# The sends of a second half chained in fours, and a quarter of the dense expert moved forward, in a decoder layer with a mixture of experts

## The chip, the cores and the metric

The kernel runs on one core of one Trainium2 chip. The metric is the time of one execution on the device in microseconds (us), the median of several runs. Lower is better. Inside a core, engines work side by side, each through its own instructions in order: PE (TensorE, matrix products; PEld is its loading of weights), DVE (VectorE), ACT (ScalarE), POOL (GpSimd) and SP (SyncE, which here issues DMAs). They wait for each other by semaphores. PEclk in the profile is the clock that TensorE was granted, as a share of the full one.

## The reference

One decoder layer over 1024 tokens of width 256 in float32: self attention, cross attention, and a mixture of experts, each behind a layer norm and with a residual. The change touches only the last:

```python
scores = softmax(xt @ Wg.T)                       # 16 experts
topi = top 4 of the experts of the best 2 of 4 groups
combine[t, topi] = scores[t, topi]
h = silu(einsum('td,eid->eti', xt, W1)) * einsum('td,eid->eti', xt, W3)   # 176 wide
y = einsum('etd,te->td', einsum('eti,edi->etd', h, W2), combine)
z = silu(xt @ Ws1.T) * (xt @ Ws3.T) @ Ws2.T       # the shared expert
return y + z
```

## The kernel before

**Tokens and halves.** The 1024 tokens are kept as eight tiles `x[i]` of 128 tokens by 256; tiles 0 to 3 are the first half, 4 to 7 the second. Routing, the shared expert and one of the 16 routed experts, the dense one (the last, `w_last`), are computed half by half. The dense expert is computed for all tokens of a half and added with each token's weight for it (`add_last`, L952), in four quarters of 256 tokens: `dense_hidden` computes the hidden layer of a quarter, `dense_output` its outputs and the adds. Before the change the two quarters of the first half are done early, and those of the second half, (1,0) and (1,1), at the end of the kernel.

**Sends.** The other 15 experts get their tokens through memory. `send` (L837) scatters the rows of a half with indirect DMAs on POOL: for each of a token's four choices k, four DMAs of 128 rows (i = 0 to 3), each row going into its expert's slots in `xd`; 16 for each half, in the order of k. `side_by_side` (L243) tells the scheduler that the sends don't depend on each other, so none waits for another. `sent_for[k]` keeps the sends of choice k.

**Experts.** The loop over e (L1353) is a software pipeline. For each expert:

- `expert_inputs(e)` loads its 384 slots (`xr`, SP queue, L1255), behind all sends of the choices 0 to min(3, e): expert 0's load waits for choice 0 alone, expert 3's and all later ones for all four. PE transposes the rows (six transposes, L1265), and ACT (L112) and DVE (L113) split them into a high and a low part, `xs`.
- `expert_weights` loads the weights (640 KB, SP queue, L277) and splits them too: a cast on ACT (L278) and subtractions on DVE or POOL (L283).
- `expert_hidden` computes 18 matmuls of 128x384, the silu on ACT (L1283, L1286), the product on DVE (L1284, L1287), and the parts `hp` of the hidden layer.
- `send_outputs` computes the outputs with 15 matmuls, copies them (L1299), and scatters them into `yd` by three indirect DMAs on POOL (L1304).

In step e of the loop, the inputs of e, the hidden layer of e − 1 and the outputs of e − 2 are written down. For e = 1 and 2 `expert_hidden` is called ahead of the next expert's inputs, and the inputs are tied behind its matmuls (`up_done`); for later e the inputs come first.

**Order.** A scheduler places the instructions on each engine, within bounds that the code gives with `tc.issue_after`. After it each engine's order is fixed.

**Tail.** `load_outputs(k)` loads the results of choice k in token order (`got`, L1320), behind all scattered outputs; nine buffers serve the sixteen loads. `add_outputs` adds them to `x` with the weights: two of three on DVE (L1334), every third scaled on ACT (L1331) and added on POOL (L1332). Between these adds stand the outputs of the dense quarters (1,0) and (1,1); the hidden layer of (1,0) is placed before the outputs of expert 14. Last, the eight tiles are written (L1392).

Of the kernel before, what the change touches and what calls it, by code (L numbers as in the profile page):

```python
# [42 lines left out]
E, INTER, NGRP, TOPK, TOPKG = 16, 176, 4, 4, 2  # L43
# [28 lines left out]
def decoder_layer(ctx: ExitStack, tc: tile.TileContext, a: dict, out: bass.AP):  # L72
# [18 lines left out]
    def av_tile():  # L91
        return ps_av.tile([128, 512], F32, tag="av", name="av")
# [18 lines left out]
    def parts_of(src, hi, lo, eng=None):  # L111
        nc.scalar.copy(hi, src)  # L112
        return (eng or nc.vector).tensor_tensor(lo, src, hi, ALU.subtract).ins  # L113
# [126 lines left out]

    yd = dram.tile([(E - 1) * SLOTS + TOPK * NT, D], F32, tag="yd", name="yd")

    def side_by_side(sent, others):  # L243

        for other in others:
            tc.declare_no_dep(sent, other, reason="each writes rows of its own")
        others.append(sent)

    def behind(read, writes):
        for w in writes:  # L250
            tc.add_manual_dep(
                read,
                w.name,
                mybir.DependencyInfo(mybir.DependencyClass.Sync, mybir.DependencyReason.DATA),
                reason="it reads rows of each",
            )
# [29 lines left out]
    def expert_up(w, xs, n):  # L286


        ps = [mm_tile(cols=n) for _ in range(3)]
        return ps, [expert_up_part(k, w, xs, t) for k, t in enumerate(ps)][-1]  # L290
# [8 lines left out]
    def expert_output(ps, w, h_p, cols):  # L299


        w2 = [[p[:, W_UP + k * D : W_UP + (k + 1) * D] for p in w] for k in range(2)]
        h = [p[:, cols] for p in h_p]
        return matmuls(
            ps,
            [
                (h[0], w2[0][0]),
                (h[0], w2[0][1]),
                (h[1], w2[0][0]),
                (h[2], w2[1][0]),  # L310
                (h[2], w2[1][1]),
            ],
        )

    with ExitStack() as attn:
# [410 lines left out]
        rows = [None, None]  # L726
        sent_rows, sent_for = [], [[] for _ in range(TOPK)]
# [108 lines left out]

        def send(half, choices=range(TOPK), waits=()):  # L837

            to = targets[half]
            for k in choices:  # L840
                for i in range(4):
                    sent = nc.gpsimd.indirect_dma_start(
                        out=xd[: TOPK * NT + (E - 1 - k) * SLOTS],
                        out_offset=bass.IndirectOffsetOnAxis(ap=to[:, k, i : i + 1], axis=0),
                        in_=rows[half][i // 2][:, i % 2, :],
                        in_offset=None,
                    ).ins
                    side_by_side(sent, sent_rows)
                    sent_for[k].append(sent)
                    behind(sent, waits)  # L850

# [107 lines left out]
        with (  # L959
# [109 lines left out]
            def dense_weights():  # L1069

                parts = [
                    xw.tile([128, 2, 2, 4 * HQ], F32R, tag=f"w_q{n}", name=f"w_last{n}")
                    .rearrange("p a b c -> p (a b c)")[:, :W_COLS]
                    for n in range(2)
                ]
                up = xb.tile([128, 3, 2, 2, DC], F32, tag="w_s", name="w_last_up")
                down = xb.tile([128, 2, D], F32, tag="w_o0", name="w_last_down")
                for t, cols in (
                    (up.rearrange("p a b c d -> p (a b c d)"), slice(0, W_UP)),
                    (down.rearrange("p a b -> p (a b)"), slice(W_UP, W_COLS)),  # L1080
                ):
                    nc.sync.dma_start(out=t, in_=a["W123"][E - 1][:, cols])
                    parts_of(t, parts[0][:, cols], parts[1][:, cols])
                return parts
# [18 lines left out]
            def dense_gated(g, up, g2, up2):  # L1103
                h_p = [
                    xa.tile([128, 512], F32R, tag=f"roped1{n}", name=f"dense1{n}", bufs=1)
                    for n in range(2)
                ]
                h_p.append(xa.tile([128, 512], F32R, tag="q_r", name="dense2"))
                nc.vector.tensor_tensor(g, up, g, ALU.mult)
                parts_of(g, h_p[0], h_p[1])  # L1110
                nc.vector.tensor_tensor(g2[:64], up2[64:], g2[64:], ALU.mult)
                parts_of(g2[:64], h_p[2][:64], h_p[2][64:])
                return h_p
# [15 lines left out]
            for n in range(len(units) + 2):  # L1129
# [5 lines left out]
                qd, half = units[min(n, len(units) - 1)]  # L1135
# [49 lines left out]
                if n == 7:  # L1185
                    choose(0)
                    send(0, (0, 1))
                if n == 8:
                    w_last = dense_weights()
                    with after(exps[-1]):  # L1190
                        routed.append(weights_of_choices(0))
                if n == 9:
# [20 lines left out]
                    with tc.issue_after(rstds[-1]):  # L1213
                        send(0, (2,), [lows[-1]])
# [8 lines left out]
                    with after(aimed, placed):  # L1223
# [4 lines left out]
                        h_p = dense_gated(*dense_ups)  # L1228
# [9 lines left out]
    gated, up_done = [None], [None]  # L1238
# [34 lines left out]
    def expert_hidden(w, xs, n):  # L1273


        ps, up_done[0] = expert_up(w, xs, n)
        g, h, g2, h2 = (
            fh.tile([128, SLOTS], F32, tag=tag, name=tag)[:, :n] for tag in ("g", "h", "g2", "h2")
        )
        h_p = [  # L1280
            fh.tile([128, SLOTS], F32R, tag=tag, name=tag)[:, :n] for tag in ("hp0", "hp1", "hp2")
        ]
        nc.scalar.activation(g, ps[0], AF.Silu)  # L1283
        nc.vector.tensor_tensor(h, ps[1], g, ALU.mult)  # L1284
        parts_of(h, h_p[0], h_p[1])
        silus.append(nc.scalar.activation(g2[64:], ps[2][:64], AF.Silu).ins)  # L1286
        nc.vector.tensor_tensor(h2[:64], ps[2][64:], g2[64:], ALU.mult)  # L1287
        gated[0] = parts_of(h2[:64], h_p[2][:64], h_p[2][64:])
        return h_p
# [37 lines left out]
    def add_outputs(k, got, cw):  # L1327
        for i in range(NI):
            y, w = got[i // 2][:, i % 2], cw[i // 4][:, k, i % 4 : i % 4 + 1]
            if i % 3 == 2:  # L1330
                nc.scalar.activation(y, y, AF.Copy, scale=w)  # L1331
                nc.gpsimd.tensor_tensor(x[i], x[i], y, ALU.add)  # L1332
            else:
                nc.vector.scalar_tensor_tensor(x[i], y, w, x[i], ALU.mult, ALU.add)  # L1334

    def dense_hidden(w, half, n):
        return expert_hidden(w, [p[:, :, n * 256 : n * 256 + 256] for p in normed[half]], 256)

    def dense_output(w, h_p, half, n, add):
        for b in range(2):  # L1340
            ps = av_tile()[:, :D]
            expert_output(ps, w, h_p, slice(b * 128, b * 128 + 128))
            add(half, 2 * n + b, ps)
# [6 lines left out]
    ws, xs, hs, got = {}, {}, {}, {}  # L1350
    with tc.issue_after(lows[-1]), tc.issue_after(silus[-1]):
        ws[0] = expert_weights(a["W123"][0], nc.vector)
    for e in range(E + 1):  # L1353
        if e in (1, 2):

            low = lows[-1]
            hs[e - 1] = expert_hidden(ws[e - 1], xs[e - 1][0], SLOTS)
        if e < E - 1:
            low = lows[-1]
            with tc.issue_after(up_done[0] if e in (1, 2) else low):  # L1360
                xs[e] = expert_inputs(e)
            if e >= 1:
                with tc.issue_after(low), tc.issue_after(silus[-1]):
                    ws[e] = expert_weights(a["W123"][e], nc.vector if e < 3 else nc.gpsimd)
        if e == 1:
            with tc.issue_after(gated[0]), tc.issue_after(silus[-1]):
                routed.append(weights_of_choices(1))
        if 0 <= e - 1 < E - 1 and e > 2:
            hs[e - 1] = expert_hidden(ws[e - 1], xs[e - 1][0], SLOTS)
        if e - 2 >= 0:  # L1370
            if e == E:

                with tc.issue_after(gated[0]):
                    h_p = dense_hidden(w_last, 1, 0)
            last = send_outputs(e - 2, ws.pop(e - 2), hs.pop(e - 2), xs.pop(e - 2)[1])
            if e - 2 == E - TOPK - 2:
                short = slots_are_short()
            k = e - 2 - (E - 1 - TOPK)
            if k >= 0:
                got[k] = load_outputs(k)  # L1380
    with ExitStack() as behind_last:
        for ins in (*last, gated[0]):
            behind_last.enter_context(tc.issue_after(ins))
        cw = [r[0] for r in routed]
        add_outputs(0, got[0], cw)
        dense_output(w_last, h_p, 1, 0, add_last)
        add_outputs(1, got[1], cw)
        dense_output(w_last, dense_hidden(w_last, 1, 1), 1, 1, add_last)
        for k in range(2, TOPK):
            add_outputs(k, got[k], cw)  # L1390
    for i in range(NI):
        (nc.sync if i % 2 == 0 else nc.scalar).dma_start(  # L1392
# [123 lines left out]
```

## Time and profile before

| | |
|---|---|
| time, median of 3 runs | 572.2 us (572.08 to 573.05) |
| the profiled execution | 577.4 us, of it 575.5 us span |
| PE busy | 540.3 us, 94% of the span |
| DVE, ACT, POOL busy | 400.2, 279.3, 230.6 us |
| share of PE in the chain that ended last | 81% |
| sends of the second half (L842), start of the first and the last | 439.40 and 460.24 us |
| loads of rows (L1255) of experts 0 to 3, issued | 446.53, 452.36, 459.83, 463.50 us |
| PE idle ahead of expert 1's first matmuls | 3.23 us |
| last stretch of DVE's adds (L1334) | from 569.50, 1.66 us |

All places in time are microseconds from the start of the span of the profiled execution, which lies 1.9 us beside its time and 5.2 us above the median of the runs. The profile gives busy times by engine, the share of each engine in the chain of work that ended last, groups of instructions by line, waits by what released them, a timeline of instructions, and the busy time by stretches of the span. A timeline line gives the start, the busy time, the engine, the line of the kernel, the operation, its output and inputs with shape, the number of instructions merged in it, and in brackets the idle time before it with its releaser. A name is that of the kernel's tile without its number; `L104` is the one line that issues every matmul, `L112` and `L113` the ones that issue the high and low parts of every split.

### The profile page before, as it was taken

What the parts mean: (1) busy time and instruction counts of PE and PEld (TensorE: products, weight loads), DVE (VectorE), ACT (ScalarE), POOL (GpSimd) and SP (SyncE); (2) the same over time, 40 slices, a digit from 0 to 9 for tenths busy, and PEclk for the clock granted to TensorE, in tenths of its full rate; (3) what the DMA queues carried; (4) which work ended last, traced back from release to release, by engine and by line L of the source; (5) the groups of instructions that cost most, each with busy time, mean ns of one, the idle gap of its engine ahead of it and who ended that gap; (6) DMA issues with size and microseconds to landing.
All of it is one profiled execution on the core that took longest, in us unless ns stands there. A gap on an engine that the chain in (4) does not pass through costs nothing.

```text
span 575.5 us, 10603 instructions
## 1 busy us (share of the span) xinstructions
PE 540.3 (94%) x4013; PEld 446.7 (78%) x4013; DVE 400.2 (70%) x879; ACT 279.3 (49%) x524; POOL 230.6 (40%) x213
## 2 busy tenths in 40 slices
PE   7999999999999989999999999999999779999962
PEld 5889898888989876757778577685787669999951
DVE  6355566644655788848577586889777479999866
ACT  4677557575574431230432323152525187777551
POOL 4260500101001005426243444632544717888862
PEclk9999999999999999999999999999999789999995
DMA  8564431823200599482020000000511658777384
GB/s 227 145 166 146 111 109 39 227 86 112 75 1 1 167 250 308 111 239 52 2 70 1 8 1 1 0 31 0 188 50 68 202 169 285 240 245 238 122 279 152
DMA packets 56294, 70.83 MB, mean 123 GB/s; under 512 B 13872, under 2 KB 42768, under 8 KB 56240
## 3 DMA queue, kind: packets, MB, share of 16 engines
q1 hardware_dynamic: 51408, 58.71, 34.5%
q0 software_dynamic: 3696, 10.36, 4.7%
q10 hardware_dynamic: 1136, 1.05, 0.6%
q8 instruction: 33, 0.54, 0.4%
q14 instruction: 21, 0.17, 0.1%
HBM read 48.61 MB, written 21.86 MB: 122 GB/s over the span
## 4 chain that ended last, share of the span: by engine, by line
PE 81%; DVE 7%; issue 4%; DMA 3%; ACT 3%; POOL 1%; SPq 1%; DVEq 0%; ACTq 0%; POOLq 0%
PE mm L104 47%; PE mm L1005 7%; PE av L590 5%; PE av L104 5%; PE at L573 4%; PE at L343 3%; PE at L1028 2%; PE av L1041 2%; PE at L1265 2%; PE mm L439 2%; DMA bqkv<-in_bqkv 1%; PE mm L461 1%; DMA got<-yd 1%; DVE x L1334 1%; POOL roped L990 1%
## 5 line engine op out<-in xcount | busy, mean ns | idle before, releaser
L990 POOL TENSOR_TENSOR roped<-rt,rt 128x512 f32<-128x512 f32 x48 | 62.6, 1325 | 83.4 <-DVE rt L984 80.5
L984 DVE TENSOR_TENSOR rt<-mm,rope_q 128x512 f32<-128x512 f32 x96 | 61.4, 685 | 24.3 <-PE mm L104 23.6
L104 PE MATMUL mm<-xn,w_q 128*128 128x512 f32 x288 | 73.9, 403 | 0.5 <-ACT xn L222 0.5
L104 PEld LDWEIGHTS mm<-xn,w_q 128*128 128x128 f32 x288 | 52.2, 188 | 14.0 <-issue 1.8
L104 PE MATMUL mm<-xs,w 128*128 128x384 f32 x270 | 55.3, 354 | 7.0 <-ACT xs L112 5.8
L1304 POOL DMA_INDIRECT yd<-y,to x45 | 47.9, 1064 | 27.6 <-ACT y L1299 13.1
L104 PEld LDWEIGHTS mm<-xs,w 128*128 128x128 f32 x270 | 48.4, 198 | 9.0 <-ACT xs L112 6.6
L327 ACT ACTIVATE p<-p 128x512 f32<-128x512 f32 x32 | 20.1, 629 | 62.3 <-DVE p L326 62.3
L324 DVE TENSOR_REDUCE sm_m<-at 128x8 f32<-128x512 f32 x32 | 21.8, 680 | 37.1 <-PE at L573 36.2
L1005 PE MATMUL mm<-roped,w_s 128*64 128x512 f32 x192 | 46.4, 602 | 0.7 <-POOL roped L990 0.7
L522 POOL TENSOR_TENSOR wv<-code,scale 128x512 fp32r<-128x512 f32 x7 | 9.5, 1360 | 88.2 <-DMA scale<-in_scales 58.7
L613 DVE TENSOR_TENSOR x<-mm,x 128x256 f32<-128x256 f32 x64 | 26.0, 419 | 23.9 <-PE mm L104 21.9
L104 PE MATMUL mm<-wo,o 128*128 128x256 f32 x256 | 39.6, 295 | 0.0
L104 PE MATMUL av<-w,hp 128*128 128x256 f32 x225 | 35.2, 290 | 0.7 <-ACT y L1299 0.7
L104 PE MATMUL mm<-xn,wq 128*128 128x512 f32 x128 | 34.6, 405 | 0.7 <-ACT xn L222 0.5
L104 PE MATMUL mm<-wv,xn 128*128 128x256 f32 x256 | 35.2, 289 | 0.0
L104 PE MATMUL mm<-xn,wk 128*128 128x512 f32 x128 | 34.9, 404 | 0.0
L590 PE MATMUL av<-pt,v 128*128 128x128 f32 x256 | 34.5, 277 | 0.0
L104 PEld LDWEIGHTS mm<-wo,o 128*128 128x128 f32 x256 | 32.9, 190 | 1.5 <-issue 0.4
L590 PEld LDWEIGHTS av<-pt,v 128*128 128x128 f32 x256 | 32.0, 191 | 1.2
L104 PEld LDWEIGHTS mm<-wv,xn 128*128 128x128 f32 x256 | 31.8, 189 | 0.9
L104 PEld LDWEIGHTS av<-w,hp 128*128 128x128 f32 x225 | 30.6, 190 | 1.9 <-ACT y L1299 1.2
(216 smaller groups left out, 1145.8 us busy)
## 6 DMA issues: line engine op xcount, KB each, us to landing
w<-in_W SPq DMA_DIRECT2D x15, 640.0 KB
code<-in_codes SPq DMA_DIRECT2D x32, 256.0 KB
scale<-in_scales SPq DMA_DIRECT2D x32, 256.0 KB
xr<-xd SPq DMA_DIRECT2D x15, 408.0 KB
xd<-zeros SPq DMA_DIRECT2D x8, 720.0 KB
yd<-zeros SPq DMA_DIRECT2D x8, 512.0 KB
got<-yd SPq DMA_DIRECT2D x16, 256.0 KB
wq<-in_Wq SPq DMA_DIRECT2D x4, 512.0 KB
```

The costliest lines, as they stand in the source:

```text
L104: m = nc.tensor.matmul(ps, lhsT=l, rhs=r, start=(n == 0), stop=(n == len(pairs) - 1))
L324: nc.vector.tensor_reduce(m, sc, AX.X, ALU.max)
L327: exps.append(nc.scalar.activation(p, p, AF.Exp, scale=scale).ins)
L343: last = nc.tensor.transpose(ps[:, 2 * n : 2 * n + 2, :].rearrange("p a q -> p (a q)"), pn[:, 2 * n : 2 * n + 2, :].rearrange("p a k -> p ...
L439: nc.tensor.matmul(ps[:, c * DCQ : (c + 1) * DCQ], lhsT=wq[:, h, c * 128 : (c + 1) * 128], rhs=wkq[:, h, :], start=True, stop=True,)
L573: nc.tensor.matmul(sc[par * 64 : par * 64 + 64, 2 * g + pp, :], lhsT=qk[0][:, b * S : (b + 1) * S], rhs=qk[1][:, b * S : (b + 1) * S], sta ...
L590: nc.tensor.matmul(av[:, k * 128 : (k + 1) * 128], lhsT=v[:, i, k0 : k0 + HD], rhs=pt[:, i].rearrange("p a q -> p (a q)"), start=True, sto ...
L613: nc.vector.tensor_tensor(x[i], ps, x[i], ALU.add)
L984: nc.vector.tensor_tensor(mt, ps3, rope_table(t, 2 * ab + k), ALU.mult)
L990: nc.gpsimd.tensor_tensor(r.rearrange("p (b s) -> p b s", s=S), one, two, op)
L1005: nc.tensor.matmul(ps[h // 2][(h % 2) * 64 : (h % 2) * 64 + 64], lhsT=w_s[:, t, blk, ab, :], rhs=roped[2 * t + ab], start=first[h], stop=l ...
L1304: sent = nc.gpsimd.indirect_dma_start(out=yd[: (E - 1) * SLOTS + min(TOPK, E - 1 - e) * NT], out_offset=bass.IndirectOffsetOnAxis(ap=to[:, ...
```

## The change

It has three parts.

1. In the second half, the first of each four sends of choices 1, 2 and 3 waits for the landing of the last send before it. `side_by_side` leaves that one dependency in. The other three of a four wait for nothing of their own, but stand behind the first in POOL's order. The first half's sends are as before.
2. The hidden layer of the dense quarter (1,0) is placed behind the matmuls of expert 0 and ahead of expert 1's transposes, and its outputs go to step e = 2, ahead of expert 0's outputs. The quarter (1,1) takes the old place of (1,0)'s hidden layer, and only its outputs stand between the adds of the tail.
3. Expert 3's inputs are placed as those of experts 1 and 2 are: behind the matmuls of the expert before.

In the built instructions, PE's order is the same up to the end of expert 0's 18 matmuls. Then come the 18 matmuls (128x256) of the dense quarter, expert 1's six transposes, and its matmuls with the quarter's ten output matmuls among them and expert 2's transposes behind them; expert 0's output matmuls, which were among expert 1's, follow after those. ACT's order after expert 0's silus has the quarter's silus ahead of the cast of expert 1's weights, and its two casts around that cast. On the SP queue the loads run: rows of 0, weights of 2, rows of 1, 2 and 3, weights of 3; before, they ran: rows of 0 and 1, weights of 2, rows of 2 and 3, weights of 3.

```diff
-    def side_by_side(sent, others):
+    def side_by_side(sent, others, landed=()):
         for other in others:
-            tc.declare_no_dep(sent, other, reason="each writes rows of its own")
+            if other not in landed:
+                tc.declare_no_dep(sent, other, reason="each writes rows of its own")
         others.append(sent)
...
             for k in choices:
+                landed = sent_rows[-1:] if half and k else ()
                 for i in range(4):
...
-                    side_by_side(sent, sent_rows)
+                    side_by_side(sent, sent_rows, landed)
...
     for e in range(E + 1):
-        if e in (1, 2):
+        if e in (1, 2, 3):
             low = lows[-1]
             hs[e - 1] = expert_hidden(ws[e - 1], xs[e - 1][0], SLOTS)
+            if e == 1:
+                with tc.issue_after(up_done[0]):
+                    h_p = dense_hidden(w_last, 1, 0)
         if e < E - 1:
             low = lows[-1]
-            with tc.issue_after(up_done[0] if e in (1, 2) else low):
+            with tc.issue_after(up_done[0] if e in (1, 2, 3) else low):
                 xs[e] = expert_inputs(e)
...
-        if 0 <= e - 1 < E - 1 and e > 2:
+        if 0 <= e - 1 < E - 1 and e > 3:
             hs[e - 1] = expert_hidden(ws[e - 1], xs[e - 1][0], SLOTS)
         if e - 2 >= 0:
             if e == E:
                 with tc.issue_after(gated[0]):
-                    h_p = dense_hidden(w_last, 1, 0)
+                    h_p = dense_hidden(w_last, 1, 1)
+            if e == 2:
+                dense_output(w_last, h_p, 1, 0, add_last)
             last = send_outputs(e - 2, ws.pop(e - 2), hs.pop(e - 2), xs.pop(e - 2)[1])
...
         add_outputs(0, got[0], cw)
-        dense_output(w_last, h_p, 1, 0, add_last)
-        add_outputs(1, got[1], cw)
-        dense_output(w_last, dense_hidden(w_last, 1, 1), 1, 1, add_last)
-        for k in range(2, TOPK):
+        dense_output(w_last, h_p, 1, 1, add_last)
+        for k in range(1, TOPK):
             add_outputs(k, got[k], cw)
```

## The prediction

> **What bounds the kernel now.** The page comes first, its busy times and its chain of work that ended last.
>
> ```profile
> PE 540.3 (94%) x4013; PEld 446.7 (78%) x4013; DVE 400.2 (70%) x879; ACT 279.3 (49%) x524; POOL 230.6 (40%) x213
> PE 81%; DVE 7%; issue 4%; DMA 3%; ACT 3%; POOL 1%; SPq 1%; DVEq 0%; ACTq 0%; POOLq 0%
> ```
>
> TensorE bounds the whole, so work can only be won where PE stands idle. The change touches two such places: the entry into the routed experts (about 440 to 475 us) and the tail (from 550). So the stretches of two microseconds come next (length, then busy time of PE, PEld, DVE, ACT, POOL, the granted clock, DMA share, GB/s).
>
> ```profile
> 448.00:450.00 2.00, 1.04 (x9) 0.84 (x8) 0.45 (x2) 0.00 (x0) 1.54 (x2) 1.00 0.83 307
> 454.00:456.00 2.00, 1.46 (x5) 1.47 (x6) 1.59 (x4) 0.96 (x2) 1.70 (x2) 0.50 1.05 303
> 460.00:462.00 2.00, 0.01 (x1) 0.00 (x0) 1.03 (x2) 1.40 (x2) 0.96 (x1) 1.00 0.70 218
> 464.00:466.00 2.00, 1.91 (x9) 1.71 (x8) 1.97 (x5) 1.66 (x2) 0.00 (x0) 0.62 0.64 193
> ```
>
> PE has holes at 449, 453 and 460 to 463, and after a hole it runs at half clock (0.50 at 454, 0.62 at 464). The timeline names what ends the holes; the bracket is the idle time before the line and its releaser.
>
> ```profile
> 446.77 1.34 PE L104 MATMUL av<-w_last,dense 128*128 128x256 f32 x10
> ...
> 448.89 0.96 POOL L842 DMA_INDIRECT xd<-rows,to  x1 [0.30 <-issue]
> 449.55 0.48 DVE L952 SCALAR_TENSOR_TENSOR x<-av,cl,x 128x256 f32<-128x256 f32 x1 [3.07 <-PE mm L104]
> ...
> 454.54 4.82 PE L104 MATMUL mm<-xs,w 128*128 128x384 f32 x18 [1.45 <-ACT xs L112]
> ...
> 459.19 0.82 PE L1265 MATMUL at<-ident,xr 128*128 128x128 f32 x6
> ...
> 461.08 1.26 ACT L278 CAST w<-w 128x1280 fp32r<-128x1280 f32 x1
> ...
> 462.70 0.48 ACT L112 CAST xs<-at 128x384 fp32r<-128x384 f32 x1 [0.37 <-remote]
> ...
> 463.24 0.79 PE L104 MATMUL mm<-xs,w 128*128 128x384 f32 x3 [3.23 <-ACT xs L112]
> ```
>
> Two things stand here. Expert 1's matmuls (463.24) wait for ACT, whose queue holds the cast of w1 ahead of the split of the rows. And what PE has finished is taken up late: the dense outputs end at 448.11 and DVE adds them at 449.55; the transposes end at 460.01 and the split starts at 462.70. Both fall into the stretch in which POOL issues send after send. The SP queue shows when each load of rows is let go, hence when the sends landed; three answers, one line each:
>
> ```profile
> 446.53 0.04 SPq L1255 DMA_DIRECT2D xr<-xd  x1
> ```
> ```profile
> 452.36 0.37 SPq L1255 DMA_DIRECT2D xr<-xd  x1
> ```
> ```profile
> 459.83 0.36 SPq L1255 DMA_DIRECT2D xr<-xd  x1
> ```
>
> Last the tail, on DVE:
>
> ```profile
> 559.50 0.42 DVE L1284 TENSOR_TENSOR h<-mm,g 128x256 f32<-128x256 f32 x1
> ...
> 560.23 0.48 DVE L952 SCALAR_TENSOR_TENSOR x<-av,cl,x 128x256 f32<-128x256 f32 x1
> ...
> 562.66 0.48 DVE L952 SCALAR_TENSOR_TENSOR x<-av,cl,x 128x256 f32<-128x256 f32 x1
> ...
> 565.25 0.97 DVE L113 TENSOR_TENSOR hp<-h,hp 64x256 fp32r<-64x256 f32 x1
> ...
> 569.50 1.66 DVE L1334 SCALAR_TENSOR_TENSOR x<-got,cw,x 128x256 f32<-128x256 f32 x4
> ```
>
> From 558.62 DVE works without a break until 571.16, and the last writes of the result follow it. Here the end is DVE's, and any DVE instruction taken out brings it forward.
>
> **Part 1: sends in fours.** It adds three waits, on the first send of choices 1, 2 and 3; behind each wait stand the other three sends of its four on POOL and nothing else that is urgent; who waits for them are the loads of rows of experts 1, 2 and 3. The price of a wait is the time from start to landing less the 1.27 us at which sends follow each other now. The trace gives a landing from the loads: last send of choice 0 at 443.51, load at 446.53 (3.0 us); choice 1, 448.89 and 452.36 (3.5); choice 2, 455.18 and 459.83 (4.65, beside a megabyte of other loads); choice 3, 460.24 and 463.50 (3.3). That is +1.75 to +3.4 each. From below: the first of all the sends, on an idle queue, landed 2.3 to 2.5 us after its start, +1.1. The Trainium skill, DMA: Bandwidth & Descriptors, Anatomy of one DMA — SWDGE (gpsimd) path, puts about 2.0 us of fixed cost on such a DMA, mostly the completion receipt: with 0.3 us of data 2.3 us, +1.0 each, and its Rules for kernel authors, to issue early and wait late, speak against waiting between sends at all. By the rule the three waits cost 3.1 us, by the rows 5 to 10. I take the rows with partial relief, as the loads beside them shift too: first sends of the three at 446.0 (+1.2), 452.4 (+2.3), 459.2 (+2.8), the last send at 463.0 and down at 465.5, so expert 3's load goes at 465.6 instead of 463.50 (+2.1) and lands near 469. Bounds of the three together: +3.3 and +10.2.
>
> On PE this costs nothing by itself: expert 1's rows come at about 457.5 where 459.2 is wanted, and expert 3's transposes are needed only at 475.7 to 477.6, which is also what part 3 amounts to (six transposes later in PE's order, 0; SP issues w2 ahead, no load more or less). The cover is 7 us; gone, it would cost the excess.
>
> A pause of POOL may be worth something: if completions are late because sends follow without pause, each four now ends in a pause of 1 to 3 us. Nothing before shows it in this place. Bounds: 0, and −2.6 (the hole of 1.65 from 449.04 to 450.68, and one more us of take-up). I take −1.0, less than the 1.65 of the one hole whose work was ready.
>
> **Part 2: a quarter of the dense expert between experts 0 and 1.** PE: 18 matmuls, 2.32 us (the row of 552.55 in the tail), and 10 output matmuls of 0.117 (10 in 1.17), 3.5 in all, moved from the tail into the middle. The quarter issues no DMA, as its weights and rows lie on the chip. The 2.32 lie in the hole of 3.23 us before 463.24. Expert 0's output matmuls, and with them its three sends of results on POOL, come some 5 us later; only the loads of the tail wait for those. Not free are the followers. On ACT two silus and two casts of the quarter (0.36, 0.38, 0.41, 0.39, the rows of the tail) stand ahead of the cast of w1 or of the rows' split: +1.54. On DVE their products and low parts likewise; beyond what ACT's delay hides, +0.46. So expert 1's main body starts 2.0 us late, 466.55 for 464.57. After that: PE's 10 output matmuls +1.17; PE's next holes, 1.10 before 471.41 and 0.27 before 472.48, are filled by that and by expert 0's outputs, which now stand there, −1.37; and the half clock. The clock is 0.5 from 464.5 to 467.9; started at 466.55, expert 1's matmuls would meet 2.0 us less of it, −1.0, if it keeps its place, nothing if it moves along; I take −0.6. Middle: 2.0 + 1.17 − 1.37 − 0.6 = +1.2. Bounds: +3.3 (3.5 of PE work less 0.2, no hole filled), and −2 (both half-clock stretches gone as well, 1.7 us each, less what ACT adds).
>
> A rule to weigh: TensorE: Matmul & The Clock Gate, Part 1, says that the clock falls after an idle window of some 3.4 us. In the trace it fell after holes of 1.65 and 3.23 us. By the rule filling a hole is worth the hole only; by the trace also the stretch behind it, in which 18 matmuls took 4.82 us where they take 3.1 at full clock: 1.7 us. The trace decides, and the −0.6 is a third of it.
>
> **Part 2 in the tail.** One quarter's hidden matmuls stay before expert 14's outputs, so PE's row of 2.32 there is unchanged, and the other quarter goes from the last stretch. DVE loses, from start to start: products 0.34 and 0.46, low parts 0.33 and 1.00, two adds 0.51 and 0.40, together 3.04. PE and ACT have room there. What could take over are the last four loads of returned rows, landed at 563.8, 564.5, 566.1 and 566.8: three adds of 0.42 behind the last two would end at 567.7, before DVE's 571.16 − 3.04 = 568.1. The writes, 2.5 us each, follow the last add. −3.0; bounds −1.0 (loads, or POOL's adds, come last) and −4.0.
>
> **Sum.** +1.2 − 1.0 − 3.0 = −2.8 us. The profiled execution has a span of 575.5 and took 577.4; the median of the runs is 572.2. The difference is applied to the median: 569.4.
>
> **Rivals.**
>
> A, the sum holds: 569.4, own range 567.5 to 570.9.
>
> B, the middle costs in full: no relief from pauses, no hole filled: +3.3 − 3.0 = +0.3, 572.5. For it: PE is at 10 of 10 in the experts that follow, so what comes in must go somewhere. Against: 3.23 us of idle PE stand just there.
>
> C, the tail gives only 1.0 because the loads or the writes end last: +1.2 − 1.0 − 1.0 = −0.8, 571.4. Against: DVE has no break in 12.5 us.
>
> D, slower: the sends now run past 463 instead of 461, so the crossings from PE to ACT and DVE for the quarter and for expert 1 all fall in the time of late take-up. The quarter adds two crossings (silu, product) ahead of the w1 cast in ACT's order. The late ones of the trace measure 1.2 (the second silu at 460.57 for matmuls done at 459.36) to 2.7 us (462.70 for 460.01). Two of 1.6 make expert 1 5.2 us late instead of 2.0; the half clock moves along (0), the pauses relieve nothing (0): 5.2 + 1.17 − 1.37 − 3.0 = +2.0, 574.2. At nought relief and clock the sum stands at −1.2, so from 1.2 us on the two crossings together the kernel is no faster, from 2.3 measurably slower. For it: the lateness grew with the number of sends. Against: fours with pauses between them.
>
> That the change doesn't do what it says is excluded for the order: in the built instructions the three waits and the moved quarter are there. Rows of expert 3 that come late would need ten us of delay, which the bounds only touch.
>
> **How the numbers follow.** A 0.52, B 0.15, C 0.05, D 0.28. A measurement of this kernel can tell about 0.2% from no change, 1.14 us: faster is below 571.06, slower above 573.34. A is faster; of C, which lies near the bound, 0.03 is faster and 0.02 the same; of B 0.13 is the same and 0.02 slower; D is slower. Faster 0.55, same 0.15, slower 0.30. The range starts at 567.0, where a tail of −4 and a middle of −1.2 would end, and reaches to 574.8, past D's middle; what is left out is D's upper half and the lowest end of A.
>
> **What would show it.** Right: first sends of the fours at 446, 452 and 459; 18 matmuls of 128x256 on PE between expert 0's and expert 1's rows, filling 460 to 463; expert 1's body 2 us later, its followers about 1 us later by expert 6; in the tail four L1284/L113 rows and two adds fewer after 558, and DVE's end 3 us earlier against the last output matmuls. Wrong: expert 1's body at 468 or later, with ACT idle before a split whose transposes were long done (D); a break of over 1 us on DVE in the tail before the last adds (C); a half-clock stretch at 467.9 to 471.3 that wasn't there (B).

## The result, and the profile after

The changed kernel takes 577.39 us in the median of 6 runs (575.55 to 578.86), the kernel before 572.62 in 6 runs beside and before it (570.88 to 574.10): the ratio is 1.0085, 95% interval 1.0062 to 1.0107, so it is slower by 4.8 us. The prediction was 569.4 and faster, with a range up to 574.8. On two of the chips of the experiments below, 39 of 102 executions of the kernel before were more than 1.5% longer than its fastest (584.9 to 589.9 us), none of the 44 with chained sends was, and the comparisons leave such executions out.

The page of the changed kernel, the same two lines:

```profile
PE 536.9 (93%) x4013; PEld 443.2 (77%) x4013; DVE 401.3 (70%) x879; ACT 279.6 (49%) x524; POOL 231.6 (40%) x213
PE 81%; DVE 8%; DMA 4%; ACT 3%; issue 2%; POOL 1%; SPq 0%; another core or an unknown queue 0%; DVEq 0%; ACTq 0%
```

Its span is 576.3 us, only 0.8 more than the 575.5 of the profile before. The medians differ by 4.8. That is the first thing to see here: the execution that was profiled before (577.4 us) was 4.8 us above its own median, and the one after (578.2) only 0.8 above its own. The two traces can't be laid side by side as they are; the experiments begin with a second profile of the kernel before.

The entry into the experts, timeline of the changed kernel (start, busy, engine, line, operation; in brackets the idle time before it and its releaser; lines are four further down than before):

```profile
446.99 1.05 POOL L846 DMA_INDIRECT xd<-rows,to  x1 [1.73 <-DMA xd<-rows,to]
...
455.77 2.31 PE L104 MATMUL mm<-xn,w_last 128*128 128x256 f32 x18
455.82 0.96 POOL L846 DMA_INDIRECT xd<-rows,to  x1 [3.48 <-DMA xd<-rows,to]
...
460.14 0.72 PE L104 MATMUL av<-w_last,hp 128*128 128x256 f32 x4 [0.90 <-ACT hp L112]
...
461.83 0.50 PE L104 MATMUL av<-w_last,hp 128*128 128x256 f32 x2 [0.45 <-DVE hp L113]
...
468.56 1.26 PE L104 MATMUL av<-w,hp 128*128 128x256 f32 x5 [1.36 <-DVE x L956]
```

The change does what it says: POOL waits for landings, and the quarter's 18 matmuls stand ahead of expert 1's rows. The three holes of the prediction (1.65, 1.45 and 3.23 us) are not in this trace, but new ones come with the quarter: its outputs wait for ACT (0.90) and DVE (0.45), and expert 0's outputs wait until DVE has added the quarter's (1.36).

The tail of the changed kernel, DVE and POOL:

```profile
561.21 5.39 DVE L1338 SCALAR_TENSOR_TENSOR x<-got,cw,x 128x256 f32<-128x256 f32 x11 [0.97 <-DMA got<-yd]
...
567.42 0.48 DVE L1338 SCALAR_TENSOR_TENSOR x<-got,cw,x 128x256 f32<-128x256 f32 x1 [0.82 <-DMA got<-yd]
...
568.07 0.73 POOL L1336 TENSOR_TENSOR x<-x,got 128x256 f32<-128x256 f32 x1 [0.78 <-ACT got L1335]
568.13 1.35 DVE L1338 SCALAR_TENSOR_TENSOR x<-got,cw,x 128x256 f32<-128x256 f32 x2 [0.22 <-DMA got<-yd]
```

DVE ends at 569.48, which is 1.7 us earlier than before (571.16), and yet the span ends later. The page doesn't count what follows: the trace's records show a closing instruction of POOL, a drain, which takes 6.36 us behind its last add, from 569.17 to 575.52, while SP has seen its last write landed and is done at 573.50. In the profile before, that drain ended at 574.19 and SP at 574.74.

### The profile page after: what moved, and what is told of

It is laid out like the page before. It is cut to its first block, busy times and chain, and to the rows that moved or that the text cites. A ratio compares the mean times of both kernels' runs of the same rounds, so it can differ in the third digit from the quotient of the medians.

```text
span 576.3 us, 10598 instructions
## 1 busy us (share of the span) xinstructions
PE 536.9 (93%) x4013; PEld 443.2 (77%) x4013; DVE 401.3 (70%) x879; ACT 279.6 (49%) x524; POOL 231.6 (40%) x213
## 4 chain that ended last, share of the span: by engine, by line
PE 81%; DVE 8%; DMA 4%; ACT 3%; issue 2%; POOL 1%; SPq 0%; another core or an unknown queue 0%; DVEq 0%; ACTq 0%
PE mm L104 47%; PE mm L1009 7%; PE av L104 6%; PE av L592 5%; PE at L575 4%; PE at L345 3%; PE at L1032 2%; PE av L1045 2%; PE mm L441 2%; DMA got<-yd 2%; PE at L1269 1%; DMA bo<-in_bo 1%; PE mm L463 1%; DMA x<-in_x 1%; POOL roped L994 1%
## 5 line engine op out<-in xcount | busy, mean ns | idle before, releaser
L988 DVE TENSOR_TENSOR rt<-mm,rope_q 128x512 f32<-128x512 f32 x96 | 61.4, 684 | 24.3 <-PE mm L104 23.6
L104 PE MATMUL mm<-xs,w 128*128 128x384 f32 x270 | 53.6, 343 | 3.2 <-issue 1.8
L329 ACT ACTIVATE p<-p 128x512 f32<-128x512 f32 x32 | 20.1, 629 | 62.3 <-DVE p L328 62.3
L104 PEld LDWEIGHTS mm<-xs,w 128*128 128x128 f32 x270 | 46.1, 190 | 5.2 <-issue 2.6
L615 DVE TENSOR_TENSOR x<-mm,x 128x256 f32<-128x256 f32 x64 | 26.0, 419 | 24.0 <-PE mm L104 22.8
```

What stands on the lines that cost most here:

```text
L104: m = nc.tensor.matmul(ps, lhsT=l, rhs=r, start=(n == 0), stop=(n == len(pairs) - 1))
L329: exps.append(nc.scalar.activation(p, p, AF.Exp, scale=scale).ins)
L615: nc.vector.tensor_tensor(x[i], ps, x[i], ALU.add)
L988: nc.vector.tensor_tensor(mt, ps3, rope_table(t, 2 * ab + k), ALU.mult)
```

## The experiments

Each ran beside the kernel before on its chip; a ratio is to that. All places are from traces of single executions.

**The kernel before, twice more.** No edit.

> The kernel before, unchanged, for a second profile of it. Both theories: time ratio 1.000 within 0.3%. The profiled execution of before took 577.4 us, 4.8 above its median, and the one of the changed kernel 578.2, 0.8 above its own; so the two traces differ by 0.8 us of span where the medians differ by 4.8. If the first profile was an unlucky execution, this one has a span near 571, and it shows which stretch was 4 us shorter: the entry into the experts (first transposes of expert 1 and 2 below 459.2 and 469.0 us) or the tail (last landing of returned rows to the end, 14.6 us in the first profile). If it again shows 575, the profiled execution is longer than the timed ones for this kernel and the traces can be compared only by their parts.

Measured: 1.0006 (0.9994 to 1.0017), span of the profile 569.0. It was the execution, or its chip: the long hole of 3.23 us isn't there.

```profile
453.41 0.85 PE L1265 MATMUL at<-ident,xr 128*128 128x128 f32 x6 [0.56 <-DMA xr<-xd]
...
455.08 0.80 PE L104 MATMUL mm<-xs,w 128*128 128x384 f32 x3 [0.82 <-ACT xs L112]
...
463.26 0.79 PE L104 MATMUL mm<-xs,w 128*128 128x384 f32 x3 [2.14 <-ACT xs L112]
```

Ahead of expert 1's matmuls TensorE now waits 0.82 us, and the longest hole, 2.14, is an expert later. A third profile of it, with three more kernels on a further chip:

> The kernel before, for a third profile. Theory V (late take-up comes in some executions, and more on some chips): ratio 1.000; its trace either starts the second half's sends near 437 and has no hole of over 1 us before expert 1 (as the second trace), or starts them near 439 to 440 and has the holes of the first trace (1.6 before expert 0's rows, 1.5 and 3.2 before experts 0's and 1's matmuls). No third picture is expected.

Measured: 0.9999 (0.9987 to 1.0011), span 569.2. It is the picture of the second but for one hole of 1.71 us, ahead of expert 1's transposes, which wait there for the rows; the expectation had none over 1 us in that place. For the rest, two groups of chips must be told apart. On three (the second profile's and two more) the second half's sends start at 436.7 to 437.4 us, and the median of before is 569.3 to 569.9 us. In all other traces, the first two among them, they start at 439.3 to 440.2; on the two further chips of the experiments most executions of before take 575 to 579 us. I call these the late chips, as what TensorE has finished is taken up late there: in the first profile ACT's split of expert 1's rows starts 2.7 us after the transposes.

**Part 1 alone, and parts 2 and 3 alone.**

```diff
 # fours_only: before with
+                landed = sent_rows[-1:] if half and k else ()
 # no_fours: the changed kernel with
-                landed = sent_rows[-1:] if half and k else ()
+                landed = ()
```

> Before with the chained sends alone (part 1); every engine's order is that of before, only the load of expert 1's rows goes behind that of expert 2's weights on the SP queue. Theory S (the sends): the second half's last send starts 6 us later (466.3 for 460.2) and the rows of experts 1 to 3 come later on a path that has nothing to hide it in the order of before: +3 to +5 us (0.5 to 0.9%). Theory Q (the quarter): the cost is the 3.5 us of TensorE work moved into the middle, with nothing won in the tail; then this kernel is within 1 us of before, or faster by up to 1 if the pauses between fours relieve the late take-up of what TensorE finished.

> The changed kernel with the second half's sends free again (parts 2 and 3 without part 1); TensorE, DVE, ACT and POOL have exactly the order of the changed kernel. Theory S: within 1 us of before or faster. Theory Q: +3.5 to +5 us against before, as the changed kernel; expert 6's first transposes no earlier than in the changed kernel. In both, the end is no earlier than POOL's last add plus about 8 us, since POOL's closing drain of 6.36 us starts behind it (569.17 to 575.53 in the changed kernel's trace).

Measured, on one chip that is not late: fours alone 1.0116 (1.0097 to 1.0136), +6.6 us; the quarter with free sends 1.0068 (1.0049 to 1.0088), +3.9 us. So both theories held in part: each part costs by itself. In the trace of the fours alone two holes carry it, ahead of the rows of expert 1 (2.57 us, where before's second trace has 0.56) and, the larger, of expert 3:

```profile
455.39 0.92 PE L1267 MATMUL at<-ident,xr 128*128 128x128 f32 x6 [2.57 <-DMA xr<-xd]
...
471.00 0.87 PE L1267 MATMUL at<-ident,xr 128*128 128x128 f32 x3 [4.68 <-DMA xr<-xd]
```

The load of expert 3's rows went at 467.54, where before's second trace has 460.52. In the trace of the quarter with free sends the holes are the quarter's own:

```profile
457.28 0.75 PE L104 MATMUL av<-w_last,hp 128*128 128x256 f32 x4 [1.40 <-ACT hp L112]
...
465.63 0.85 PE L104 MATMUL av<-w,hp 128*128 128x256 f32 x5 [2.13 <-DVE x L952]
```

TensorE's idle time from 436 to 483 us is 5.5 us in before's second trace and 5.9 here. The quarter's 3.5 us of matmuls came in, and no idle time went out in return.

**Fours with part 3, the quarter left in the tail** (two chips, neither late).

```diff
 # before with part 1 and
-        if e in (1, 2):
+        if e in (1, 2, 3):
... (and the two conditions that go with it)
```

> Before with the chained sends and with expert 3's rows placed behind expert 2's matmuls (parts 1 and 3, the quarter left where it was). The chained sends alone measured +6.6 us, and in their trace TensorE stood idle for 4.68 us ahead of expert 3's transposes at 471.00, whose rows were loaded at 467.54 behind a last send 5.8 us later than in before. If that hole is the price of the fours, the later place takes most of it away: +1.5 to +2.5 us against before. If the price is in the rows of experts 1 and 2 and in the pauses themselves: still +5 to +6.5.

> Chained sends and expert 3's rows later, the quarter left in the tail, on the same chip. Where before has no late take-up: +1.9 us, as measured (1.0033). Where it has it: faster than before by 2 to 4 us, if the chained sends do relieve it; +1.9 again if they do not.

Measured: 1.0033 (1.0020 to 1.0046) and 1.0038 (1.0023 to 1.0052), +1.9 and +2.2 us. The later place of expert 3's rows takes some 4.5 us off the price of the fours. What is left stands in front of the rows of experts 1 and 3:

```profile
455.41 0.84 PE L1267 MATMUL at<-ident,xr 128*128 128x128 f32 x6 [2.51 <-DMA xr<-xd]
...
471.24 0.85 PE L1267 MATMUL at<-ident,xr 128*128 128x128 f32 x6 [1.67 <-DMA xr<-xd]
```

Part 3, which I had costed at nothing, is what makes part 1 bearable. Neither kernel ran on a late chip, so what part 1 by itself does there is untested.

**The tail alone.** The quarter (1,0) left out altogether, then also with the last choice's adds all on DVE; and that second edit on before and on the changed kernel.

```diff
 # quarter_out: before without dense_hidden/dense_output of (1, 0)
 # last_dve:
-            if i % 3 == 2:
+            if i % 3 == 2 and k < TOPK - 1:
                 nc.scalar.activation(y, y, AF.Copy, scale=w)
                 nc.gpsimd.tensor_tensor(x[i], x[i], y, ALU.add)
```

> Before without the quarter (1,0) of the dense expert altogether: its hidden layer, its outputs and its adds are left out, and the quarter (1,1) has the place that it has in the changed kernel. This is the tail part of the change by itself. The sum of the prediction had -3.0 us for it, from DVE's work. Theory D: POOL's drain sets the end, and DVE's freed time is not used: -1.5 to 0 us against before. The difference of this kernel to the one with free sends and the moved quarter (+4.0) is then the price of the quarter in the middle: +4 to +5.5 us, where the prediction had +1.2.

> Before without the quarter (1,0), as the kernel beside it, and with the adds of the last choice all on DVE. Theory D: with the drain out of the way the freed DVE time does count: -2.5 to -3.5 us against before. If the limit were the landing of the last loads of returned rows, which both kernels share: no more than 1 us below the kernel with the quarter left out alone.

Measured: 0.9995 (0.9984 to 1.0005), then 0.9941 (0.9928 to 0.9954). Without the quarter the kernel is no faster, −0.3 us; with POOL's last adds gone as well it is 3.4 us faster. POOL's last rows of the two:

```profile
557.03 1.82 POOL L1332 TENSOR_TENSOR x<-x,got 128x256 f32<-128x256 f32 x2 [1.51 <-ACT got L1331]
```
```profile
554.79 0.73 POOL L1332 TENSOR_TENSOR x<-x,got 128x256 f32<-128x256 f32 x1 [0.54 <-ACT got L1331]
```

POOL ends at 558.85 and 555.51, its drain at 565.32 and 561.99, SP at 562.82 and 562.31, the spans at 566.1 and 563.1; DVE ends at 559.5 and 559.4. In the first the drain ends last, 2.5 us behind SP; in the second SP does, 0.3 us behind the drain. What POOL's adds wait for in the first is not DVE: each takes a row that ACT has scaled, and ACT waits for the loads of returned rows (us in all, times, longest):

```profile
ACT got L1331 <- DMA got<-yd: 8.9, 6, 2.8
```

So DVE's freed time does not move the end until POOL's last adds are gone. (The profiled execution of the first is 3 us shorter than before's, with a drain that ends 2.9 us earlier, its median only 0.6; single traces of this kernel differ by more than the effects here, so the verdicts are those of the medians.)

> The changed kernel, with the adds of the last choice all on DVE: two scale-and-add pairs on ACT and POOL become two DVE adds of 0.42 us. If POOL's closing drain sets the end, as the trace of the changed kernel shows (drain from 569.17 to 575.53, all else done at 573.50), it now starts about 4 us earlier, and the end moves to that of the DVE adds and the last writes: -1.0 to -2.0 us against the changed kernel, so +2.8 to +3.8 against before. If the drain is not what sets the end, or waits for the last writes anyway: within 0.5 us of the changed kernel or slower by the 0.8 us of added DVE work.

> Before, with the adds of the last choice all on DVE instead of every third on ACT and POOL. Theory D (POOL's closing drain of 6.36 us behind its last add sets the end): in the second trace of before the drain ended at 568.19 and SP's last wait at 566.17; the drain now starts 4 us earlier, DVE's end moves from 563.18 by two adds, 0.84, so the end is SP's at about 567.0 plus 0.8: -1.2 us against before (0.9979), down to -0.4 if an execution has DVE late as the first trace had. If the drain is no limit: +0.8 us from the added DVE work.

Measured: on the changed kernel 1.0058 (1.0035 to 1.0080) where the changed kernel by itself stands at 1.0085, about −1.5 us, but with intervals that overlap and not on one chip; on before 0.9998 (0.9987 to 1.0010), nothing. There the drain and SP end within 2 us of each other (568.19 and 566.17 in the second trace, 567.77 and 568.41 in the third); that each becomes the limit as soon as the other gives way fits this, and isn't shown further. A second way to start the drain early, with POOL's adds moved from the last choice to the choices before it:

```diff
-            if i % 3 == 2:
+            if k < TOPK - 1 and (i % 3 == 2 or (k and i == 7)):
```

> Before, with POOL's and ACT's share of the adds (8 of 32) moved to the choices 0 to 2 and none in the last choice; DVE has as many adds as before. POOL's closing drain starts some 4 us earlier without more work for DVE, so the end is SP's last wait instead of the later of the two: in the second trace of before they stood at 568.19 (drain) and 566.17, in the third at 567.77 and 568.41. So 0 to -2 us, -1.0 in the mean (0.9983) against before; the edit that gave DVE two adds more measured -0.1. If the last loads of returned rows set DVE's end: 0.

Measured, on a late chip: 1.0052 (1.0032 to 1.0071), slower by 3 us. The edit missed its aim: POOL's last add, of tile 7, stood behind the dense quarter's add to the same tile (idle 4.55 us, released by DVE L952), so the drain started no earlier (569.11).

**The quarter elsewhere.** Its hidden layer behind expert 2's transposes (`turned` is the last of them), where before's second trace has the hole of 2.14 us; free sends and the last adds on DVE, and (1,1) alone in the tail, as in the change.

```diff
                 xs[e] = expert_inputs(e)
+            if e == 2:
+                with tc.issue_after(turned[0]):
+                    h_p = dense_hidden(w_last, 1, 0)
...
+            if e == 3:                            # 4 in the second kernel
                 dense_output(w_last, h_p, 1, 0, add_last)
```

> Free sends; the quarter's hidden layer behind expert 2's transposes instead of ahead of expert 1's, its outputs among expert 3's matmuls, and the adds of the last choice on DVE. In the second trace of before the one long hole of TensorE in the entry is 2.14 us ahead of expert 2's matmuls (463.26), where ACT has the cast of w2 before the split of the rows; ahead of expert 1's it is 0.56 and 0.82. Theory H (the quarter cost +4.3 because where it was put the holes are short, and its own outputs wait there): here 2.1 of its 2.3 us are covered, and the middle costs 1.2 for the outputs and 0.2 to 0.8 more; with the tail's -3.4 that makes -1.4 to -2.0 us against before (0.9965 to 0.9975), a version faster than both kernels. Theory P (what comes into the middle is paid in full wherever it goes, as ACT and DVE pass its parts ahead of the experts' own): +3.5 to +4.3 in the middle, 0 to +1 against before.

> The quarter behind expert 2's transposes with free sends and the last adds on DVE, on the same chip. Theory H, where before has no late take-up: -1.4 to -2.0 us, as expected before; it measured +1.3 us (1.0023) on a chip where before took 579 us and where late take-up hit this kernel too. Theory P: 0 to +1 us on any chip.

> As the kernel beside it, with the quarter's outputs one expert later, among expert 4's and 5's matmuls, so that they wait for nothing. Theory H: within 0.5 us of the kernel beside it. If the outputs' own waits are a good part of the price, this one is faster by 0.5 to 1 us.

> Parts 2 and 3 of the change with free sends, and the adds of the last choice on DVE: the quarter at the change's own place with the tail's limit taken away. The tail alone is worth -3.4 us then, and the middle costs +4.3: +0.5 to +1.5 us against before. If the tail's gain does not add to the rest: +3 or more, as without that edit.

Measured on a chip that is not late: 1.0012 (0.9999 to 1.0024), +0.7 us. Theory H had −1.4 to −2.0 and is wrong in the sum; theory P's 0 to +1 holds. In the trace expert 2's hole is gone, and others stand behind it:

```profile
464.33 0.52 PE L1265 MATMUL at<-ident,xr 128*128 128x128 f32 x3 [0.88 <-DMA xr<-xd]
...
468.04 2.18 PE L104 MATMUL mm<-xs,w 128*128 128x384 f32 x11 [0.83 <-DVE w L283]
```

Taken with the tail's −3.4, the quarter costs 4.1 us here too. Where, the traces leave open: from the start of the sends to the last output matmul of the routed experts it is 110.8 us here, 108.8 and 108.9 in the two later profiles of before and 107.7 without the quarter and with the same tail; from there to the end it is 20.2 us here and 18.6 without the quarter. So 2.0 to 3.2 us of the price lie in the middle, and 1.5 behind it.

On a late chip the same kernel gave 1.0023 (1.0002 to 1.0044), the one with the later outputs 1.0003 (0.9973 to 1.0033), the quarter at the change's place with the last adds on DVE 1.0116 (1.0082 to 1.0149). The latter's trace has holes of 3.15 and 9.43 us in the entry, so it says nothing of the tail.

**The changed kernel on both kinds of chip, and the relief.**

> The changed kernel, unchanged, on the same chip as the kernels with one part: +4.8 us against before (1.0085). The chained sends with part 3 alone gave +1.9 and the quarter with part 3 alone +4.0; if the two prices added up, it would be +5.9. Its profile should show the start of the sends at 437 instead of 440.1, and expert 6's first transposes about 4 to 6 us later than before's second trace (481.63).

> The changed kernel on the same chip. If before's executions here have no late take-up: +4.8 to +6 us (1.008 to 1.010), the sum of what its parts cost on the chips without it. If they have it: 0 to +2 us, as the chained sends then save most of what they cost (+0.8 us was measured where before took 579 us).

Measured: on a late chip 1.0013 (0.9994 to 1.0033); on one that is not, 1.0088 (1.0057 to 1.0118), +5.0 us. The traces of the late chip show why the change is nearly free there. First TensorE with free sends (the kernel with the quarter behind expert 2's transposes), then the changed kernel:

```profile
451.51 0.74 PE L104 MATMUL mm<-ws,sh 96*128 96x256 f32 x4 [1.63 <-issue]
...
454.63 4.74 PE L104 MATMUL mm<-xs,w 128*128 128x384 f32 x18 [1.72 <-DVE x L948]
...
462.69 0.80 PE L104 MATMUL mm<-xs,w 128*128 128x384 f32 x3 [2.66 <-issue]
```
```profile
452.91 1.01 PE L104 MATMUL mm<-xs,w 128*128 128x384 f32 x3 [0.83 <-DVE x L952]
454.28 2.88 PE L104 MATMUL mm<-xs,w 128*128 128x384 f32 x15 [0.36 <-DVE xs L113]
...
461.62 0.74 PE L104 MATMUL av<-w_last,hp 128*128 128x256 f32 x4 [1.66 <-ACT hp L112]
```

With free sends the holes are those of the first profile (1.6, 1.5 to 1.7, 2.5 to 3.2), and expert 0's 18 matmuls take 4.74 us, with a granted clock of 0.50 from 454.2 to 457.6. The five traces of free sends on late chips all have such holes, two of them (executions of 586 and 589 us) longer ones. None of the three with chained sends has them: 0.2 to 0.8 us ahead of expert 0's matmuls, which take 3.7 to 3.9, and 0.9 to 1.7 where the quarter's outputs wait for ACT. In one of the two long traces, of the quarter at the change's place with free sends, ACT splits expert 0's rows 8.9 us after their transposes, behind the last of the sends:

```profile
452.77 0.82 PE L1265 MATMUL at<-ident,xr 128*128 128x128 f32 x6
...
459.21 0.96 POOL L842 DMA_INDIRECT xd<-rows,to  x1 [0.30 <-issue]
...
462.49 0.86 ACT L112 CAST xs<-at 128x384 fp32r<-128x384 f32 x2 [15.34 <-remote]
```

The times agree: the fastest of this kernel's 22 executions took 580.4 us, the fastest of the changed kernel's 22 on the same chip 577.5. The two differ in the sends and in the last adds, which cost nothing elsewhere (1.0058 for 1.0085, and 0.9998).

**Expert 3's weights ahead of its rows on the SP queue.**

```diff
 # the changed kernel, e == 3
+                    ws[e] = expert_weights(a["W123"][e], nc.gpsimd)
+            with tc.issue_after(up_done[0] if e in (1, 2, 3) else low), tc.issue_after(w_loads[-1] if e == 3 else low):
                 xs[e] = expert_inputs(e)
... (w_loads: the weight loads so far; the later call for e == 3 is left out)
```

> The changed kernel with two loads exchanged on the SP queue: the weights of expert 3 ahead of its rows, all other orders as in the changed kernel. In the traces of the changed kernel the weights were issued right behind the rows (at 467.5 and 468.9 us where the sends started at 437; 464.3 to 464.7 in before), since the rows' load stood in the queue waiting for the last of the chained sends. Theory W (a part of the price is that weights queue behind waiting rows): issued near 462 to 463 now, their cast no longer late, holes before expert 3's matmuls of 0.6 to 3.5 us gone: -1 to -3 us against the changed kernel, +2 to +4 against before (1.0035 to 1.007). Theory M (the price is the 3.5 us of the quarter's TensorE work and the rows themselves): within 0.5 us of the changed kernel, 1.0085.

Measured, on a late chip: 1.0023 (1.0008 to 1.0039), where the changed kernel had 1.0013 (0.9994 to 1.0033) on another late chip. The load went at 462.3 instead of 469.8 and 469.4 in the two traces of the changed kernel on late chips (the places in the expectation, 467.5 and 468.9, were those of expert 4's weights behind it), and expert 6's transposes start 1.4 and 1.8 us sooner after the first send than in those (47.4 us for 48.8 and 49.2), but the medians show no gain. Inconclusive: the two never ran on one chip.

## Why the prediction was wrong

Times from the start of the second half's first send, in us; an expert is turned where its first transpose starts:

| trace | last send | rows of 3 loaded | expert 6 turned | expert 14 turned | end |
|---|---|---|---|---|---|
| before, second / third | 20.4 / 20.3 | 23.5 / 23.7 | 44.6 / 44.7 | 90.5 / 90.6 | 132.0 / 132.6 |
| fours alone | 26.2 | 30.5 | 51.1 | 96.9 | 138.1 |
| fours and part 3 | 26.3 | 30.4 | 46.5 | 92.1 | 132.2 |
| quarter, free sends | 20.1 | 23.6 | 48.7 | 95.0 | 135.0 |
| changed, third | 26.2 | 28.8 | 47.4 | 93.7 | 133.4 |
| before, first (late chip) | 20.8 | 24.1 | 48.7 | 94.6 | 136.1 |
| changed, first (late chip) | 26.2 | 28.8 | 48.8 | 95.0 | 136.2 |

- **"The 2.32 lie in the hole of 3.23 us."** This step failed first. The hole came of the late take-up in the profiled execution: in the second and third profile 0.82 and 0.24 us stand there. I had seen that this execution stood 5.2 us above the median, and only moved the sum over to the median; I should have asked where those 5.2 us lay. The second and third profile are 6.5 and 6.3 us shorter: 2.4 and 2.7 of that lie ahead of the sends, 4.0 between the first send and expert 14, where the holes stand that I meant to fill.
- **Middle +1.2.** It is the quarter's price with free sends less the tail alone, 1.0068 − 0.9995, or 4.2 us. That is the 3.5 us of TensorE work and some waits of its own. My bound of +3.3 (rival B) came nearest, and was still short. That ACT and DVE pass the quarter's parts ahead of the experts' was in the sum; that the quarter's outputs and their adds then hold up TensorE, whose order is fixed (1.40 and 2.13 us with free sends), was not.
- **Tail −3.0.** Measured −0.3. DVE's work did leave, and 3.4 us are to be had once POOL's last adds go; but POOL's drain ended 0.55 us before SP in the first trace, and 2.0 us after it in the second. "Here the end is DVE's" was the wrong step: I read the end from DVE's last add and did not ask what the 4.4 us behind it were. POOL's last add waits for loads and ACT, and 6.36 us of drain follow it.
- **Fours: 0, relief −1.0.** The last send came 5.8 us later, where I had 2.8, less than my own lower bound of 3.3; the rows of the trace (5 to 10 us for three waits) were right, and the 3.1, my estimate from the Trainium skill, DMA: Bandwidth & Descriptors, Anatomy of one DMA — SWDGE (gpsimd) path, was too little. The rule of the same page to wait late (Rules for kernel authors) stood against this part, and was right on the chips without late take-up: +1.9 to +2.2 us even with part 3. "Expert 1's rows come at about 457.5 where 459.2 is wanted" leaned on the late execution too: with fours and part 3 on the other chips TensorE stands ready 2.5 us before expert 1's rows come (0.6 and 1.7 in the later profiles of before), and 1.7 before expert 3's. On late chips there is a relief, and it is larger than the 1.0 that I took: from the start of the sends to expert 14's rows, the kernel before loses 4.0 us there against the other chips (94.6 for 90.5), and the changed one 1.3 (95.0 for 93.7), in single traces.
- **"No load more or less" on the SP queue.** The count was right, the times were not: expert 3's weights stand behind its rows as before, the rows wait longer, and the weights went 5.4 us later (466.6 for 461.2 on the third chip).
- **On the kind of chip that was profiled.** In the first trace of before the last output matmul of the routed experts ends 113.3 us after the second half's first send, in the first trace of the changed kernel also 113.3; middle and relief had +0.2. From there to the end it is 22.8 and 22.9; the tail had −3.0. So there the tail is the whole miss, and the middle came out by luck: by the prices on the other chips the quarter and the fours cost more than I took, and the relief gave more.
- **Rivals.** B's middle and C's reason for the tail held together, with the fours' price on top: 4.2 − 0.3 + 2.0 = +5.9, where 5.0 was measured on a chip that is not late. D had the wrong mechanism: with chained sends take-up on late chips was earlier, not later.

What stays open: where, on the third chip, the medians' 5.0 us lie, as the traces of the changed kernel and of before differ by 1.1 only. The traced execution of the changed kernel was the shortest of its four (572.1 us, median 574.3), that of before the longest of its twelve (571.1, median 569.5); one hole that comes and goes is in front of expert 3's matmuls (0.64 us there, 3.50 in the kernel with the last adds on DVE). What makes a chip late, and whether the first 571 to 574 us of before, the profile of 577.4 and the first runs of the changed kernel came from one chip, isn't known; so the first ratio may mix kinds of chip, and 1.0088 and 1.0013 are the ratios by kind. No version here beat both kernels; the nearest is before with the last adds on DVE, at 0.9998.

## What to carry to other kernels

When the profiled execution is longer than the median, find where the excess lies before counting on any hole in it, and take a second profile. Work moved into a stretch where the chain runs through every engine can bring waits of its own; in this kernel it was paid in full at both places. An end is reached when the last engine is through its closing work: compare all engines' ends with the end of the span before pricing what one of them saves.

## What the hardware showed that I had not expected

- POOL's drain after its last instruction took 6.36 us in all twenty traces, and the page doesn't list it. Where POOL's last add came late (it ends at 568.8 in the first trace of the changed kernel), this drain ended last (575.52).
- On some chips, what TensorE finished was taken up late while POOL issued sends one after the other (1.2 to 2.7 us in the first profile, 8.9 in a long execution); the traces with pauses behind every four sends have none of those holes. The mechanism isn't shown.
- In the tail, beside loads of 256 KB each, the last indirect DMA landed 3.4 to 5.3 us after its start (548.62 to 553.58 in the third profile of before), against 2.6 us from the last of the chained sends to the load that waits for it (463.12 to 465.71 in the changed kernel on the third chip).
